# Attention scores with neighbours on partitions, and two gates that each form their own u3 product, in a two-layer graph network

## The chip, the core and the metric

The kernel runs on one core of a Trainium2 chip. The metric is the time of one execution on the device, in microseconds (us). Beside the time of each run there is a profile of one execution, which records what every engine did: TensorE (PE, with its weight loads, PEld), VectorE (DVE), ScalarE (ACT), GpSimd (POOL) and the queues that issue DMAs (SP and ACT here).

## What is computed

The input x holds 32 samples of 512 nodes with 128 features, all in 32-bit floats. One 512 x 512 adjacency matrix of zeros and ones, with a full diagonal, serves all samples. Layer 0 is a graph attention, layer 1 a gated network that runs five steps; both begin with a layer norm and a ReLU, and both add their result to x.

```python
# layer 0
h = relu(layernorm(x)); hw = h @ W
e_src = hw @ a_src; e_dst = hw @ a_dst
logits = leaky_relu(e_src[:, :, None] + e_dst[:, None, :], 0.2)
alpha = softmax(logits + where(A > 0, 0.0, -1e9), axis=-1)
x = x + leaky_relu(alpha @ hw + b, 0.3)
# layer 1: h = relu(layernorm(x)), then five times
m = A @ h                          # the same for both halves of av
u3 = h @ u3_w.T + u3_b
z = sigmoid(av @ w3_w.T + w3_b + u3)
r = sigmoid(av @ w4_w.T + w4_b + u3)
hv = tanh(av @ w5_w.T + w5_b + (r * h @ u5_w.T + u5_b))
h = (1 - z) * h + z * hv
# at last: x = x + h
```

Since in_matrix and out_matrix are the same, both halves of av are m, and the kernel adds the two halves of each weight once at its start. A sigmoid is formed from a tanh of half its argument.

## The kernel before

A sample's 512 nodes lie as 128 partitions of K = 4 nodes each. All matrix work is in 32-bit floats. PSUM is used as eight banks of 128 x 512, handed out in turn under one tag by `bank(name)` (line 62).

The preparation (lines 98 to 170) loads the adjacency matrix and the weights, writes the additive mask of layer 0 with four DVE operations (line 131), turns the matrix into `adjT` with sixteen transposes (line 142) and sums and turns the gate weights (lines 151 to 167). For the gates it forms w4 and, in `w3dT`, the difference of w3 and w4.

`layer0(b)` (lines 202 to 280) is a generator. It does one piece of a sample's layer 0 and gives control back at each `yield`, twelve pieces in all:

- layer norm on DVE, with the inverse root on POOL (`relu_layernorm`, line 177);
- four transposes into one PSUM bank and a copy by ACT (`transposed`, line 194);
- h W with one further column for e_src (line 217), and a product that gives e_dst on every partition (line 222); ACT adds each node's e_src to it, four times 128 x 512 (line 227);
- six pieces (lines 233 to 265) with the nodes that receive on partitions. For each group of 128 nodes: the leaky ReLU (line 237), mask and row maximum in one DVE operation (line 240), its sign turned (line 244), the exponential with its row sum (line 246), four transposes of the result and a copy (lines 197 and 198), and four products with hw (line 258). A group's exponential, transposes and products are one piece apart;
- division by the row sum and bias (line 270), the leaky ReLU and the sum with x (lines 275 and 276);
- the second layer norm, and at the end its transposes.

The main loop (lines 389 to 412) runs 160 passes, one for each sample and step. A pass starts `aggregate` for one item (four products, line 289, and the copy to `mT` by ACT), `gate_r` for the item of the pass before, `candidate` and `update` for the one before that, and then `turn` (four transposes, line 338) for the last. Between these it calls `advance()` three times, and each call does one piece of layer 0 for a sample that is still to come. At most six samples are in the loop (WIDTH); twelve have space for their state (SLOTS). The first six samples go through layer 0 before the loop, two side by side (`start_first`, line 370). When no sample is left for layer 0 the loop runs on alone, and the last two samples alternate.

Both gates need u3 h. `gate_r` starts one PSUM bank with it (line 300), adds w4 m (line 301), and ACT reads the bank for r (line 303). `candidate` then adds (w3 - w4) m to the same bank (line 311), so that ACT reads z from it (line 315). A pass thus has nine products of 512 columns.

The calls are emitted in this order, and the framework's scheduler puts them into one queue per engine. An engine works through its queue in order.

Of the kernel before, what the change touches and what calls it, by code (L numbers as in the profile page):

```python
# [17 lines left out]
NEG = -1000000000.0  # L18
WIDTH = 6
SLOTS = 12  # L20


@with_exitstack
def gat_then_gated_gnn_kernel(
# [29 lines left out]
    const = ctx.enter_context(tc.tile_pool(name="const", bufs=1))  # L54
    state = ctx.enter_context(tc.tile_pool(name="state", bufs=1))
# [28 lines left out]
    mask = const.tile([P, K, N], F32, name="mask")  # L84
    wsrc = const.tile([P, D + 1], F32, name="wsrc")
    wdst = const.tile([P, P], F32, name="wdst")
    bias0 = const.tile([P, D], F32, name="bias0")
    nc.scalar.dma_start(out=bias0, in_=g_b.partition_broadcast(P))
    w3dT = const.tile([P, D], F32, name="w3dT")
# [8 lines left out]
    with tc.tile_pool(name="prep", bufs=1) as prep:  # L98
# [28 lines left out]
        nc.vector.tensor_scalar(wdst, ones, wa[:, 1:2], None, ALU.mult)  # L127


        for k in range(K):  # L130
            nc.vector.tensor_scalar(
                mask[:, k, :].rearrange("p (c q) -> p c q", c=K),
                a_sb[:, k, :].rearrange("p (q c) -> p c q", c=K),
                0.0,
                NEG,
                ALU.is_le,
                ALU.mult,
            )
# [12 lines left out]
        sums = {}  # L151
        for name in ("w4", "w3", "w5"):
            sums[name] = prep.tile([P, D], F32, name=name + "s")
            nc.vector.tensor_tensor(sums[name], wide[name][:, :D], wide[name][:, D:], ALU.add)
        nc.vector.tensor_tensor(sums["w3"], sums["w3"], sums["w4"], ALU.subtract)
        for name, dst in (("w3", w3dT), ("w4", w4sT), ("w5", w5sT)):
            ws = sums[name]
            t_ps = bank(name + "_ps")
            nc.tensor.transpose(t_ps[:, :D], ws, ident)
            nc.vector.tensor_copy(dst, t_ps[:, :D])  # L160
# [13 lines left out]
    hNs = [state.tile([P, K, D], F32, name=f"hN_{s}") for s in range(SLOTS)]  # L174

# [26 lines left out]
    def layer0(b):  # L202
# [9 lines left out]
        hw = w2.tile([P, K, D + 1], F32, tag="hw", name=f"hw_{b}")  # L212
        for half in range(K // 2):
            hp = bank(f"hp_{b}_{half}")
            hp2 = hp[:, : 2 * (D + 1)].rearrange("p (c e) -> p c e", c=2)
            for c in range(2):
                nc.tensor.matmul(  # L217
                    hp2[:, c, :], lhsT=hT[:, ts(2 * half + c, P)], rhs=wsrc, start=True, stop=True
                )
            nc.scalar.copy(hw[:, 2 * half : 2 * half + 2, :], hp2)  # L220
        ed = bank(f"ed_{b}")
        nc.tensor.matmul(ed, lhsT=wdst, rhs=hT, start=True, stop=True)  # L222
        sums = w2.tile([P, K], F32, tag="sums", name=f"sums_{b}")
        s_all = []
        for k in range(K):
            s = w2.tile([P, N], F32, tag=f"s{k}", name=f"s_{b}_{k}", bufs=1)
            nc.scalar.activation(s, ed, AF.Identity, bias=hw[:, k, D : D + 1])
            s_all.append(s)
        yield

        probs, turned = {}, {}
        av = None
        for i in range(K + 2):
            if i < K:
                s = s_all[i]
                lg = w2.tile([P, N], F32, tag="lg", name=f"lg_{b}_{i}")
                nc.vector.scalar_tensor_tensor(lg, s, 0.2, s, ALU.mult, ALU.max)
                ml = w2.tile([P, N], F32, tag="ml", name=f"ml_{b}_{i}")
                top = w3.tile([P, 1], F32, tag="top", name=f"top_{b}_{i}")
                nc.vector.tensor_tensor_reduce(  # L240
                    ml, lg, mask[:, i, :], 1.0, -3.0e38, ALU.add, ALU.max, top
                )
                ntop = w3.tile([P, 1], F32, tag="ntop", name=f"ntop_{b}_{i}")
# [145 lines left out]
    while ready or waiting or coming or current or any(pipeline):  # L389
# [8 lines left out]
        if pipeline[1]:  # L398
            gate_r(*pipeline[1])
# [44 lines left out]
```

## Time and profile before

| what | value |
|---|---|
| time, median of 3 runs (lowest to highest) | 1699.15 us (1698.23 to 1699.98) |
| the profiled execution's own time | 1699.15 us |
| its span, first to last instruction | 1697.2 us |
| mean granted clock of TensorE, as a share of full speed | 0.979 |
| DVE busy | 943.7 us (56%) |
| ACT busy | 706.9 us (42%) |
| POOL busy | 79.3 us (5%) |
| x, one sample's load, issue to landing (median) | 2.6 us |
| out, one sample's store, issue to landing (median) | 2.0 us |

In a line of the groups, the form is: source line, engine, operation, names of output and inputs, shapes, count, then total busy time in us and the mean of one in ns, then idle time ahead of it and what ended it. In a timeline the first two columns are the start and the length in us. The lengths of matmuls overlap[...]. The times in a profile are those of one execution; the prediction is a sum against that execution's time.

### The profile page before, as it was taken

The numbers are of one execution on the slowest core, as the hardware profiler recorded it, in microseconds if no ns is written. First come the engines' busy times: TensorE is split into PE (matmuls) and PEld (weight loads), VectorE is DVE, ScalarE is ACT, GpSimd is POOL, SyncE is SP. The second block draws the span as 40 slices with busy tenths as digits, with TensorE's granted clock in tenths as the row PEclk, the third lists the DMA queues.
The fourth block names the chain that finished last, engine by engine and source line by source line (L and its number), as shares of the span: only waits on it lengthen the run. The fifth ranks groups of instructions, "written<-read, shape, count | busy, mean of one in ns | idle before, by whom it ended". The sixth has DMA issues, their size and how long they took to land.

```text
span 1697.2 us, 15921 instructions
## 1 busy us (share of the span) xinstructions
PE 1597.3 (94%) x5656; PEld 860.7 (51%) x5656; DVE 943.7 (56%) x2455; ACT 706.9 (42%) x1285; POOL 79.3 (5%) x70
## 2 busy tenths in 40 slices
PE   5557999999999999999999999999999999999987
PEld 4444555554555555455555545555554554444433
DVE  5665666664666665466666546666663654433433
ACT  4443444443444443344444334444443443333322
POOL 0000000000000000000000000000000000000000
PEclk9768999999999999999999999999999999999999
DMA  1000000000000000000000000000000000000100
GB/s 60 13 13 13 7 7 8 11 7 7 32 13 7 7 7 7 7 31 13 7 7 7 7 7 31 13 7 7 7 0 7 25 7 0 1 0 0 38 0 13
DMA packets 11456, 19.50 MB, mean 11 GB/s; under 512 B 2161, under 2 KB 3057, under 8 KB 11249
## 3 DMA queue, kind: packets, MB, share of 16 engines
q1 hardware_dynamic: 10080, 18.35, 3.3%
q8 instruction: 44, 0.72, 0.2%
q10 hardware_dynamic: 1296, 0.14, 0.1%
q14 instruction: 36, 0.29, 0.1%
HBM read 10.10 MB, written 8.39 MB: 11 GB/s over the span
## 4 chain that ended last, share of the span: by engine, by line
PE 80%; DVE 14%; POOL 3%; ACT 1%; issue 1%; DMA 0%; POOLq 0%; ACTq 0%
PE m L289 28%; PE v L318 7%; PE g L300 7%; PE v L317 7%; PE g L301 7%; PE av L258 7%; PE g L311 6%; PE h L338 4%; PE t_p L197 4%; POOL rs_b L187 3%; DVE hN L189 2%; DVE o L270 2%; PE hp L217 2%; PE ed L222 2%; DVE st_b L181 1%; DVE x L276 1%
## 5 line engine op out<-in xcount | busy, mean ns | idle before, releaser
L289 PE MATMUL m<-adjT,hN 128*128 128x512 f32 x1280 | 578.1, 594 | 7.4 <-DVE hN L341 7.4
L289 PEld LDWEIGHTS m<-adjT,hN 128*128 128x128 f32 x1280 | 231.5, 191 | 240.2 <-issue 230.9
L305 DVE SCALAR_TENSOR_TENSOR rh<-rs,hT 128x512 f32<-128x512 f32 x160 | 110.2, 689 | 360.3 <-ACT rs L303 360.2
L293 ACT COPY mT<-m 128x512 f32<-128x512 f32 x160 | 93.8, 586 | 503.1 <-PE m L289 503.1
L329 DVE TENSOR_TENSOR d<-hv,hT 128x512 f32<-128x512 f32 x160 | 109.4, 684 | 176.9 <-ACT hv L326 176.9
L303 ACT ACTIVATE rs<-g,rb 128x512 f32<-128x512 f32 x160 | 109.6, 685 | 173.4 <-PE g L301 173.4
L326 ACT ACTIVATE hv<-v,vb 128x512 f32<-128x512 f32 x160 | 110.1, 688 | 148.7 <-PE v L318 148.7
L311 PE MATMUL g<-mT,w3dT 128*128 128x512 f32 x320 | 163.6, 593 | 0.0
L300 PE MATMUL g<-hT,u3T 128*128 128x512 f32 x320 | 163.5, 592 | 0.0
L317 PE MATMUL v<-mT,w5sT 128*128 128x512 f32 x320 | 163.5, 592 | 0.0
L318 PE MATMUL v<-rh,u5hT 128*128 128x512 f32 x320 | 163.4, 592 | 0.0
L301 PE MATMUL g<-mT,w4sT 128*128 128x512 f32 x320 | 163.4, 592 | 0.0
L258 PE MATMUL av<-hw,pt 128*128 128x128 f32 x1024 | 137.6, 279 | 0.0
L258 PEld LDWEIGHTS av<-hw,pt 128*128 128x128 f32 x1024 | 129.5, 196 | 13.0 <-issue 12.7
L315 ACT ACTIVATE zs<-g,zb 128x512 f32<-128x512 f32 x160 | 110.0, 687 | 44.4 <-PE g L311 43.7
L341 DVE COPY hN<-h 128x512 f32<-128x512 f32 x128 | 87.8, 686 | 69.7 <-PE h L338 69.7
L331 DVE SCALAR_TENSOR_TENSOR e<-zs,d 128x512 f32<-128x512 f32 x160 | 110.4, 690 | 3.6
L332 DVE SCALAR_TENSOR_TENSOR hT<-e,hT 128x512 f32<-128x512 f32 x160 | 109.9, 687 | 3.1
L338 PEld LDWEIGHTS h<-ident,hT 128*128 128x128 f32 x640 | 77.2, 141 | 49.9 <-issue 34.7
L197 PEld LDWEIGHTS t_p<-ident,pe 128*128 128x128 f32 x512 | 65.6, 147 | 72.5 <-issue 41.1
L338 PE MATMUL h<-ident,hT 128*128 128x128 f32 x640 | 96.5, 273 | 4.4 <-DVE hT L332 4.4
L301 PEld LDWEIGHTS g<-mT,w4sT 128*128 128x128 f32 x320 | 60.8, 190 | 76.5 <-issue 76.5
(85 smaller groups left out, 1448.3 us busy)
## 6 DMA issues: line engine op xcount, KB each, us to landing
x<-in_x_dram SPq DMA_DIRECT2D x32, 256.0 KB, 2.6
out_dram<-res SPq DMA_DIRECT2D x32, 256.0 KB, 2.0
a_sb<-in_adj_dram SPq DMA_DIRECT2D x1, 1024.0 KB, 8.2
w<-in_L_gnn_w_w_dram SPq DMA_DIRECT2D x3, 128.0 KB, 2.3
u<-in_L_gnn_u_w_dram SPq DMA_DIRECT2D x2, 64.0 KB, 2.3
bias<-in_L_gnn_b_dram ACTq DMA_DIRECT2D x1, 64.0 KB, 6.1
gw<-in_L_gnn_W_dram ACTq DMA_DIRECT2D x1, 64.0 KB, 8.4
cols<-in_L_gnn_w_b_dram ACTq DMA_DIRECT2D x3, 0.5 KB, 6.3
```

Of the source, the lines that this page charges most:

```text
L197: nc.tensor.transpose(t[:, ts(k, P)], src[:, k, :], ident)
L258: nc.tensor.matmul(av[:, ts(k, P)], lhsT=pt[:, ts(c, P)], rhs=hw[:, c, :D], start=(c == 0), stop=(c == K - 1),)
L289: nc.tensor.matmul(m_ps, lhsT=hN[:, k, :], rhs=adjT[:, k, :], start=(k == 0), stop=(k == K - 1))
L300: nc.tensor.matmul(g_ps, lhsT=u3T, rhs=hT, start=True, stop=False)
L301: nc.tensor.matmul(g_ps, lhsT=w4sT, rhs=mT, start=False, stop=True)
L305: nc.vector.scalar_tensor_tensor(rh, r, 1.0, hT, ALU.add, ALU.mult)
L311: nc.tensor.matmul(g_ps, lhsT=w3dT, rhs=mT, start=False, stop=True, skip_group_check=True)
L317: nc.tensor.matmul(v_ps, lhsT=w5sT, rhs=mT, start=True, stop=False)
L318: nc.tensor.matmul(v_ps, lhsT=u5hT, rhs=rh, start=False, stop=True)
L326: nc.scalar.activation(hv, v_ps, AF.Tanh, bias=vb)
L331: nc.vector.scalar_tensor_tensor(e, z, 1.0, d, ALU.add, ALU.mult)
L338: nc.tensor.transpose(t[:, ts(k, P)], hT[:, ts(k, P)], ident)
```

## The change

Layer 0 forms its scores with the sending nodes (the neighbours) on partitions. The logit of a pair is the larger of s and 0.2 s, with s = e_src + e_dst. Its exponential is the larger of exp(s) and exp(0.2 s). Divided by exp(0.2 e_src), which is the same for all neighbours of a node and so cancels in the softmax, it is the larger of exp(0.8 e_src + e_dst) and exp(0.2 e_dst). ACT forms the first for 128 neighbours against all 512 nodes, and the second as one number per neighbour (`low`). One DVE operation takes the larger and multiplies by the transposed adjacency matrix, which is there already for layer 1. The result has the layout that the product with hw needs. The row sums come from a further column of ones in hw, so the products have 130 columns. The row maxima, the mask and the transposes of the scores go. Twelve pieces stay twelve.

The gates form u3 h twice: each gate has its own PSUM bank and its own u3 product, and w3 takes the place of w3 - w4. Both gates are done where r alone was, and `candidate` becomes part of `update`.

The short form of the scores holds for an adjacency matrix of zeros and ones with a neighbour for each node, and for scores that aren't large. The preparation computes from the inputs a flag that says whether this is broken. At the end of the program each engine reads the flag and branches: where it is set, `general_path` computes everything once more, in a loop over the samples, with mask and row maxima.

```diff
-    mask = const.tile([P, K, N], F32, name="mask")
+    wrow = const.tile([P, D + 1], F32, name="wrow")
+    wcol = const.tile([P, P], F32, name="wcol")
+    flag = const.tile([P, 1], mybir.dt.int32, name="flag")
...
-        for k in range(K):
-            nc.vector.tensor_scalar(
-                mask[:, k, :].rearrange("p (c q) -> p c q", c=K),
-                a_sb[:, k, :].rearrange("p (q c) -> p c q", c=K),
-                0.0,
-                NEG,
-                ALU.is_le,
-                ALU.mult,
-            )
+        nc.vector.tensor_copy(wrow[:, :D], gw)
+        nc.vector.tensor_copy(wrow[:, D : D + 1], wa[:, 1:2])
+        nc.vector.tensor_scalar(wcol, ones, wa[:, 0:1], None, ALU.mult)
...
+        odd = prep.tile([P, K, N], F32, name="odd")
+        nc.vector.scalar_tensor_tensor(
+            odd, a_sb, 0.0, a_sb, ALU.not_equal, ALU.not_equal, accum_out=viol[:, 0:1]
+        )
+        nc.vector.tensor_reduce(deg, a_sb, mybir.AxisListType.X, ALU.max)
+        nc.vector.tensor_scalar(bare, deg, 0.0, None, ALU.is_le)
+        nc.vector.tensor_reduce(viol[:, 1:2], bare, mybir.AxisListType.X, ALU.add)
+        nc.vector.tensor_tensor(wa2, wa, wa, ALU.mult)
+        nc.vector.tensor_reduce(viol[:, 2:3], wa2, mybir.AxisListType.X, ALU.add)
+        viol_ps = bank("viol_ps")
+        nc.tensor.matmul(viol_ps[:, 0:3], lhsT=ones, rhs=viol, start=True, stop=True)
+        nc.vector.tensor_scalar(over, viol_ps[:, 2:3], SCORES, None, ALU.is_gt)
+        nc.vector.tensor_reduce(total, viol_ps[:, 0:2], mybir.AxisListType.X, ALU.add)
+        nc.vector.tensor_tensor(total, total, over, ALU.add)
+        nc.vector.tensor_scalar(flag, total, 0.0, None, ALU.is_gt)
...
+    hws = [state.tile([P, K, D + 2], F32, name=f"hw_{s}") for s in range(3)]
+    for t in hws:
+        nc.vector.memset(t[:, :, D + 1 : D + 2], 1.0)
...
-        ed = bank(f"ed_{b}")
-        nc.tensor.matmul(ed, lhsT=wdst, rhs=hT, start=True, stop=True)
-        for k in range(K):
-            nc.scalar.activation(s, ed, AF.Identity, bias=hw[:, k, D : D + 1])
+        es = bank(f"es_{b}")
+        nc.tensor.matmul(es, lhsT=wcol, rhs=hT, start=True, stop=True)
+        low = w2.tile([P, K], F32, tag="low", name=f"low_{b}")
+        nc.scalar.activation(low, hw[:, :, D], AF.Exp, scale=0.2)
         yield
-        for i in range(K + 2):
...
-                nc.vector.tensor_tensor_reduce(
-                    ml, lg, mask[:, i, :], 1.0, -3.0e38, ALU.add, ALU.max, top
-                )
...
-                transposed(pt, probs.pop(i - 1).rearrange("p (c q) -> p c q", c=K), f"p{b}_{i}")
...
-            yield
+        for c in range(K):
+            e = w2.tile([P, N], F32, tag="e0", name=f"e0_{b}_{c}")
+            nc.scalar.activation(e, es, AF.Exp, bias=hw[:, c, D : D + 1], scale=0.8)
+            pt = w2.tile([P, N], F32, tag=f"pt{c}", name=f"pt_{b}_{c}")
+            nc.vector.scalar_tensor_tensor(
+                pt, e, low[:, c : c + 1], adjT[:, c, :], ALU.max, ALU.mult
+            )
+            probs.append(pt)
+            yield
+        for half in range(K // 2):
+            av = bank(f"av_{b}_{half}")
+            av2 = av[:, : 2 * (D + 2)].rearrange("p (c e) -> p c e", c=2)
+            for i in range(2):
+                k = 2 * half + i
+                for c in range(K):
+                    nc.tensor.matmul(
+                        av2[:, i, :],
+                        lhsT=probs[c][:, ts(k, P)],
+                        rhs=hw[:, c, :],
+                        start=(c == 0),
+                        stop=(c == K - 1),
+                    )
+            nc.vector.reciprocal(rsum[:, 2 * half : 2 * half + 2], av2[:, :, D + 1])
+            for i in range(2):
+                k = 2 * half + i
+                nc.vector.scalar_tensor_tensor(
+                    o[:, k, :], av2[:, i, :D], rsum[:, k : k + 1], bias0, ALU.mult, ALU.add
+                )
+            yield
...
-    def gate_r(b, step):
+    def gate(b, step):
         hT, mT = hTs[b % SLOTS], aggregates[b]
-        g_ps = bank(f"g_{b}_{step}")
-        nc.tensor.matmul(g_ps, lhsT=u3T, rhs=hT, start=True, stop=False)
-        nc.tensor.matmul(g_ps, lhsT=w4sT, rhs=mT, start=False, stop=True)
+        for name, wT, bias, pool in (("r", w4sT, rb, w2), ("z", w3sT, zb, w3)):
+            g_ps = bank(f"{name}_{b}_{step}")
+            nc.tensor.matmul(g_ps, lhsT=u3T, rhs=hT, start=True, stop=False)
+            nc.tensor.matmul(g_ps, lhsT=wT, rhs=mT, start=False, stop=True)
+            g = pool.tile([P, N], F32, tag=name, name=f"{name}s_{b}_{step}")
+            nc.scalar.activation(g, g_ps, AF.Tanh, bias=bias, scale=0.5)
...
-    def candidate(b, step):
-        nc.tensor.matmul(
-            g_ps, lhsT=w3dT, rhs=mT, start=False, stop=True, skip_group_check=True
-        )
...
+    ctx.close()
+    general = nc.values_load(flag[0:1, 0:1])
+    with tc.If(general > 0):
+        with ExitStack() as inner:
+            general_path(
+                inner,
+                tc,
+                x,
+                adj,
+                (ident, wsrc, wdst, bias0, w3sT, w4sT, w5sT, u3T, u5hT, zb, rb, vb),
+                out,
+            )
```

The new function, cut to its frame:

```python
def general_path(ctx, tc, x, adj, ws, out):
    ...
    with tc.For_i(0, B, 1) as b:
        nc.sync.dma_start(out=xb, in_=...)
        relu_layernorm(h, xb, "a")
        ...
        for i in range(K):
            ...
        for step in range(STEPS):
            ...
        nc.sync.dma_start(out=..., in_=hN)
```

## The prediction

> **What bounds the kernel now.** I read the page's busy shares first, then the groups by line, then busy time by stage, and last the timeline of each stage.
>
> ```profile
> span 1697.2 us, 15921 instructions
> ...
> PE 1597.3 (94%) x5656; PEld 860.7 (51%) x5656; DVE 943.7 (56%) x2455; ACT 706.9 (42%) x1285; POOL 79.3 (5%) x70
> ...
> PEclk9768999999999999999999999999999999999999
> ```
>
> TensorE (PE) is busy 94% of the span, so what the change does to PE decides, unless a stage waits for something else. PEclk is full from the fourth slice on; only the start runs at a reduced clock.
>
> ```profile
> L289 PE MATMUL m<-adjT,hN 128*128 128x512 f32 x1280 | 578.1, 594 | 7.4 <-DVE hN L341 7.4
> ...
> L300 PE MATMUL g<-hT,u3T 128*128 128x512 f32 x320 | 163.5, 592 | 0.0
> ...
> L258 PE MATMUL av<-hw,pt 128*128 128x128 f32 x1024 | 137.6, 279 | 0.0
> ...
> L197 PE MATMUL t_p<-ident,pe 128*128 128x128 f32 x512 | 81.1, 284 | 13.5 <-ACT pe L246 13.5
> ```
>
> x1280 for the 640 products of line 289 shows that each f32 product is two MATMUL records, and a transpose (line 197) is one. The mean of a record, 592 ns, is not its price in a stream, since records overlap. The price is read from start to start in the timeline of a steady stretch:
>
> ```profile
> 258.90 0.66 PE L197 MATMUL t_b<-ident,hN 128*128 128x128 f32 x4 [0.65 <-DVE hN L192]
> 259.39 0.60 PE L338 MATMUL h<-ident,hT 128*128 128x128 f32 x4
> 259.83 3.60 PE L289 MATMUL m<-adjT,hN 128*128 128x512 f32 x8
> 263.27 1.02 PE L300 MATMUL g<-hT,u3T 128*128 128x512 f32 x2
> 264.12 1.02 PE L301 MATMUL g<-mT,w4sT 128*128 128x512 f32 x2
> ...
> 274.48 0.60 PE L197 MATMUL t_p<-ident,pe 128*128 128x128 f32 x4
> 274.92 1.02 PE L311 MATMUL g<-mT,w3dT 128*128 128x512 f32 x2
> ...
> 277.93 1.06 PE L258 MATMUL av<-hw,pt 128*128 128x128 f32 x8
> 278.82 0.60 PE L338 MATMUL h<-ident,hT 128*128 128x128 f32 x4
> ```
>
> From 263.27 to 264.12 one product of 512 columns takes 0.86 us; four of them (line 289) 3.44; four transposes 0.44 (274.48 to 274.92); four products of 128 columns 0.89 (277.93 to 278.82), so 0.22 each. Nothing stands idle but 0.65 us before t_b, which waits for VectorE (DVE).
>
> By stages:
>
> ```profile
> 0.00:140.57 140.57, 72.91 (x421) 62.30 (x421) 84.96 (x338) 58.52 (x124) 14.47 (x19) 0.77 0.10 30
> 140.57:391.71 251.14, 247.12 (x920) 135.25 (x920) 150.67 (x422) 114.88 (x216) 15.55 (x13) 0.99 0.02 7
> 391.71:416.21 24.50, 24.50 (x68) 11.44 (x67) 10.10 (x15) 7.95 (x13) 0.00 (x0) 1.00 0.00 1
> 416.21:1614.15 1197.94, 1183.74 (x4072) 620.88 (x4071) 669.07 (x1638) 504.39 (x902) 49.25 (x39) 1.00 0.03 11
> 1614.15:1697.20 83.05, 69.06 (x180) 30.79 (x180) 28.87 (x43) 21.19 (x32) 0.00 (x0) 0.98 0.02 7
> ```
>
> Columns are stage, its length, then busy time of PE, PE's weight loads, DVE, ScalarE (ACT), GpSimd (POOL), then clock and DMA. The start (0 to 140.57) keeps PE half busy at clock 0.77. From there to 1614.15 PE is full at a full clock. From 391.71 to 416.21 no layer-0 work runs: three passes of the main loop take 24.50, so 8.17 each, which is nine products (7.73) and four transposes (0.44). With layer 0 beside it, the chain of waits shows the same POOL line at 214.19, 255.66 and 297.13: one sample of layer 0 per four passes, in 41.47 us. The sum 140.57 + 26 x 41.47 + 48 x 8.17 = 1611 against 1614.15 confirms this division (26 samples are left after the first six; 160 passes less 104 and less 8 in the end). In the end two samples alternate, and a round takes 19.3 us, in which PE also waits:
>
> ```profile
> 1633.53 3.70 PE L289 MATMUL m<-adjT,hN 128*128 128x512 f32 x8 [1.00 <-DVE hN L341]
> ...
> 1647.13 1.02 PE L318 MATMUL v<-rh,u5hT 128*128 128x512 f32 x2
> ...
> 1652.83 3.70 PE L289 MATMUL m<-adjT,hN 128*128 128x512 f32 x8 [1.00 <-DVE hN L341]
> ```
>
> And in the start two samples go through layer 0 side by side; from the first score operation to the sum with x is 21.8 us (65.52 to 87.34), 21.0 for the third pair (108.62 to 129.65):
>
> ```profile
> 65.52 2.42 ACT L227 ACTIVATE s<-ed,hw 128x512 f32<-128x512 f32 x4 [1.12 <-PE ed L222]
> ...
> 87.34 0.68 DVE L276 TENSOR_TENSOR x<-x,o 128x512 f32<-128x512 f32 x1
> ```
>
> [...]
>
> **The change part by part.**
>
> *The second u3 product.* Each of 160 passes gets one more 512-column product. In 48 free passes nothing else changes: 48 x 0.86 = +41.3. The other engines follow: DVE has five and ACT four operations of 0.69 in a pass of 9.03.
>
> *Layer 0 in 26 periods.* Added: four products, 3.44. Removed: sixteen transposes of scores in four groups, 4 x 0.44 = 1.76. The sixteen products for the output go from 128 to 130 columns: 0.22 x 2/128 x 16 = 0.06. Products of 129 columns (line 217) already take 0.89 for four, as those of 128 do, so an odd width has no price. Sum +1.74. The 0.65 before t_b: t_b waits for the second layer norm, whose DVE chain begins when the last output product ends. The built order keeps between the two one aggregate, four gate products and two of the candidate, 3.44 + 6 x 0.86 = 8.6 us of PE, as before, but only two of the four operations on the output (0.3 each) remain behind that product, because the other half comes earlier. So the wait shrinks to between 0 and 0.65; I take -0.25. But this wait can grow too, if an operation of the main loop (0.69) is put into that chain: rh is one, in the built order it stands ahead of the ReLU; the upper end is +1. Taken: +1.5 per period, 26 x 1.5 = +39.
>
> *Work off PE that goes.* Per sample DVE loses 4 x (0.68 + 0.69 + 0.08 + 0.15) and gets 4 x 0.69; ACT loses four biased copies, four evacuations and the sums, and keeps four exponentials of about 0.69. DVE was busy 121 of 200 us and ACT 92, both beside a full PE: worth nothing in these periods. The four exponentials stand together in ACT's built order, and the third waits until DVE has used the first (two buffers). Behind them ACT holds the copy of the aggregate, needed by PE one pass later (9 us), and DVE holds rh, also needed a pass later: hidden. A PSUM bank returns after eight requests; the fuller loop asks 27 times per period instead of 26, and the scores' bank is read within the four exponentials, so I see no wait there.
>
> *The end.* In a round PE now does both gates of both samples before the first candidate. The loop from candidate (1647.13) to the next aggregate (1652.83) stays 5.70, and three added products lie ahead of it (the u3 products of both, and the second sample's z moved forward): +2.58 a round for three rounds, and +1.72 at the last, where the second sample ends the kernel: +9.5.
>
> *The start.* The score stage of a pair is now a chain of eight exponentials and eight multiplications that alternate over two buffers. ACT and DVE both take 0.69, and the rhythm comes to about 0.7 us each; the second sample's scores product comes 1.75 after the first (0.89 + 0.86). First exponential to last multiplication: about 7.2. Then PE has twenty output products left, of which fifteen lie ahead of the first sample's second half: 3.3 at full clock, 6.6 at half. Reciprocal, two operations and the leaky ReLU, 0.17 + 0.6 + 0.7 = 1.5. In all 12 to 15 against 21.0 and 21.8: 6 to 10 less for a pair; taken 8[...]. Layer norms, loads and transposes of x between pairs stay (19 us from 89.45 to 108.62). The first pair pays for the preparation: the mask (2.17) goes; two passes over 2048 columns come. No row shows them; the nearest is 0.61 per 512 columns, so 2.5 and about 2.2. About ten small operations of 0.1 to 0.3 follow, and the built order puts all of these ahead of the first normalisation on DVE, which came at 13.80 and will come near 20.5; its successors were held by PE until 19.35 anyhow. Net +4.5 (3 to 6). Together 4.5 - 3 x 8 = -19.5, with ends -9 and -27.
>
> *The flag and the branch.* For these inputs it is false: the matrix holds 0 and 1 with a full diagonal, and the squared sum of the two score vectors is near 128 x 2 x 0.01 = 2.6, below 25; so the general path costs only its skipping. Every engine reads the flag and branches at the end of its queue. [...] Taken +2.
>
> *At no cost.* The three hw tiles and the memsets (before x has landed at 6.6), the small exponential (ahead of its scores product on ACT), the same DMAs in SP's queue, POOL unchanged.
>
> *Sum.* 41.3 + 39 + 9.5 - 19.5 + 2 = +72.3. The profiled execution took 1699.15 with a span of 1697.2, and is the median of the runs shown; so 1771.
>
> **Rivals.** *The start gives nothing back*: half clock throughout and a longer preparation. For it: clock 0.53 at 100 to 110; against: DVE and ACT have 12 us less in each pair's stage. 1771 + 19 = 1790.
> *A new wait in each period*: ACT stops in the middle of its exponentials for DVE, and something behind it reaches PE late. For it: strict order in both queues; against: a slack of a pass. At 1.5 us: 26 x 1.5 = +39, 1810.
> *Faster*: the removed transposes were worth their records' 273 ns each and not 0.11, because each group interrupts the stream. Then 416 of them give 113.6 rather than 45.8, and 1771 - 68 = 1703, with the start at its best (-27) 1696. It decides from 1.14 us for a group of four on. Against: groups of 0.44 in the timeline at every place.
> *The skip is dear*[...]: +20, 1791.
>
> **How the numbers follow.** Forecast 1771: 0.70; start gives nothing back 0.12; new wait 0.10; skip dear 0.05; faster 0.03. A measurement of this kernel tells 0.2% (3.4 us). Unknowns about the forecast: start -8 to +10, the wait before t_b -10 to +26, the end of the program -2 to +4: 1755 to 1798 covers the forecast, the first rival and the dear skip; the new wait and the faster case stay out. Faster by over 0.2%: 0.02; within: 0.01; slower: 0.97.
>
> **What would show it.** Lines for u3 with 640 records; a free pass of 9.03 us; a period near 43.0; a round near 21.9; the first aggregate near 121. Wrong if periods are under 41.5, if PE has idle time before the gates, or if the general path's lines appear in the trace.

## The result and the profile after

| | before | after |
|---|---|---|
| time, median (lowest to highest), 4 runs each | 1698.95 us (1698.23 to 1699.98) | 1757.76 us (1756.75 to 1758.56) |
| ratio to before, 95% interval | | 1.0345 (1.0327 to 1.0363) |
| span of the profiled execution | 1697.2 us | 1755.3 us |
| first aggregate of the main loop starts at | 140.57 us | 119.64 us |
| a free pass (no layer 0 beside it) | 8.17 us | 9.02 us |
| a period (one sample of layer 0, four passes) | 41.47 us | 42.30 us |
| a round of the end | 19.3 us | 21.8 us, two of 23.4 us |

The kernel became 3.5% slower, 58.8 us by the medians and 58.1 by the spans. The forecast was 1771 with a range of 1755 to 1798. The direction and the place of the loss were right; the loss was forecast 13 us too large. Where a time stands below without a range, that kernel ran once; those with a range ran four or five times and spread by at most 2.6 us.

The page of the profile after:

```profile
span 1755.3 us, 14839 instructions
...
PE 1674.0 (95%) x5466; PEld 870.1 (50%) x5466; DVE 886.1 (50%) x2115; ACT 568.4 (32%) x933; POOL 65.1 (4%) x70
...
PEclk9679999999999999999999999999999999999998
...
L457 PE MATMUL r<-mT,w4sT 128*128 128x512 f32 x320 | 163.4, 592 | 0.0
L456 PE MATMUL r<-hT,u3T 128*128 128x512 f32 x320 | 163.4, 592 | 0.0
L456 PE MATMUL z<-hT,u3T 128*128 128x512 f32 x320 | 163.4, 592 | 0.0
L457 PE MATMUL z<-mT,w3sT 128*128 128x512 f32 x320 | 163.4, 592 | 0.0
```

DVE has lost 58 us of work and ACT 139, and the kernel is slower all the same: the engine that counts, PE, has 77 us more. Line 456, the u3 product, stands there twice with 320 records each, 640 in all. The last digit of PEclk is an 8 where before had a 9: the end of the kernel now has something that slows TensorE.

The same stages as before (stage, length, then busy time of PE, weight loads, DVE, ACT, POOL, clock, DMA):

```profile
0.00:119.64 119.64, 59.31 (x326) 48.49 (x327) 74.85 (x284) 31.67 (x58) 13.18 (x19) 0.78 0.12 34
119.64:377.68 258.04, 257.31 (x874) 135.94 (x874) 139.69 (x356) 89.82 (x151) 12.70 (x13) 0.99 0.02 7
377.68:404.75 27.07, 27.07 (x73) 12.57 (x73) 10.10 (x15) 7.95 (x13) 0.00 (x0) 1.00 0.00 1
404.75:1657.70 1252.95, 1250.87 (x4000) 637.73 (x4000) 632.69 (x1418) 417.80 (x681) 39.25 (x39) 1.00 0.03 10
1657.70:1755.30 97.60, 79.46 (x196) 35.34 (x196) 28.78 (x43) 21.19 (x32) 0.00 (x0) 0.93 0.02 6
```

The start is 20.9 us shorter. The loop, from the first aggregate to the end rounds, has grown from 1473.58 to 1538.06, +64.5; the end from 83.05 to 97.60, +14.5. Together +58.1. In the three free passes PE is busy 27.07 of 27.07. The new thing is the second row: PE is busy 257.31 of 258.04, where before had 247.12 of 251.14. The same holds for the fourth row (2.1 us idle, 14.2 before). So an idle time of PE that stood in every period of before is gone. The list of waits (who waited, for whom, us in total, times, longest) shows which. Before, then after:

```profile
PE t_b L197 <- DVE hN L192: 46.4, 31, 7.9
```

```profile
PE t_b L365 <- DVE hN L360: 28.3, 6, 7.2
```

Six of these waits belong to the six samples of the start. The other 25 of before, one in nearly every period, do not exist any more.

How the layer norm that t_b waits for lies in each kernel is read in the timeline (start, length, engine; only lines of that chain are kept). Before, the last output product having ended at 290.7:

```profile
294.86 0.69 DVE L276 TENSOR_TENSOR x<-x,o 128x512 f32<-128x512 f32 x1
...
297.10 0.68 DVE L305 SCALAR_TENSOR_TENSOR rh<-rs,hT 128x512 f32<-128x512 f32 x1
297.13 1.50 POOL L187 TENSOR_TENSOR rs_b<-ve_b,mhalf 128x4 f32<-128x4 f32 x1 [34.14 <-DVE ve_b L185]
...
299.91 0.41 DVE L192 TENSOR_SCALAR hN<-hN 128x512 f32<-128x512 f32 x1
...
300.38 0.66 PE L197 MATMUL t_b<-ident,hN 128*128 128x128 f32 x4 [0.65 <-DVE hN L192]
```

After, where it ended at 231.9:

```profile
234.73 0.69 DVE L431 TENSOR_TENSOR x<-x,o 128x512 f32<-128x512 f32 x1
...
237.00 1.01 POOL L355 TENSOR_TENSOR rs_b<-ve_b,mhalf 128x4 f32<-128x4 f32 x1 [37.36 <-DVE ve_b L353]
...
239.28 0.68 DVE L463 SCALAR_TENSOR_TENSOR rh<-rs,hT 128x512 f32<-128x512 f32 x1
239.87 0.42 DVE L360 TENSOR_SCALAR hN<-hN 128x512 f32<-128x512 f32 x1
...
240.73 0.60 PE L365 MATMUL t_b<-ident,hN 128*128 128x128 f32 x4
```

From the end of the output products to the end of the ReLU it is 9.6 us before (290.7 to 300.32) and 8.4 after (231.9 to 240.29). PE has the same work in between in both: a turn 0.44, an aggregate 3.44, six products 5.16, together 9.0. So before t_b came 0.8 us late in each period (the product ahead of it started at 298.71 and a stream would have gone on at 299.57; as idle time 0.65 is shown). In after its input is done 0.44 us ahead of it: its bracket has no wait. The 1.2 us are made of 1.3 less for outputs behind the last product, 0.5 less on GpSimd (1.50 to 1.01), and 0.6 more because rh now stands ahead of the ReLU.

### The profile page after: what moved, and what is told of

Its sections match the earlier page's. It is cut to its first block, busy times and chain, and to the rows that moved or that the text cites. A ratio compares the mean times of both kernels' runs of the same rounds, so it can differ in the third digit from the quotient of the medians.

```text
span 1755.3 us, 14839 instructions
## 1 busy us (share of the span) xinstructions
PE 1674.0 (95%) x5466; PEld 870.1 (50%) x5466; DVE 886.1 (50%) x2115; ACT 568.4 (32%) x933; POOL 65.1 (4%) x70
## 4 chain that ended last, share of the span: by engine, by line
PE 94%; DVE 4%; POOL 1%; ACT 1%; DMA 0%; issue 0%; ACTq 0%; POOLq 0%; DVEq 0%
PE m L444 32%; PE r L456 8%; PE r L457 8%; PE z L457 8%; PE z L456 8%; PE v L470 8%; PE v L471 8%; PE av L414 6%; PE h L485 4%; PE hp L385 2%; PE es L390 2%; PE t_a L365 1%; PE t_b L365 1%; DMA gw<-in_L_gnn_W_dram 0%; DVE pt L401 0%; DVE hN L357 0%
## 5 line engine op out<-in xcount | busy, mean ns | idle before, releaser
L459 ACT ACTIVATE rs<-r,rb 128x512 f32<-128x512 f32 x160 | 109.9, 687 | 180.9 <-PE r L457 180.9
L457 PE MATMUL r<-mT,w4sT 128*128 128x512 f32 x320 | 163.4, 592 | 0.0
L456 PE MATMUL r<-hT,u3T 128*128 128x512 f32 x320 | 163.4, 592 | 0.0
L456 PE MATMUL z<-hT,u3T 128*128 128x512 f32 x320 | 163.4, 592 | 0.0
L457 PE MATMUL z<-mT,w3sT 128*128 128x512 f32 x320 | 163.4, 592 | 0.0
L459 ACT ACTIVATE zs<-z,zb 128x512 f32<-128x512 f32 x160 | 110.0, 687 | 164.7 <-PE z L457 164.7
L414 PEld LDWEIGHTS av<-hw,pt 128*128 128x128 f32 x1024 | 124.2, 190 | 33.8 <-issue 25.1
L414 PE MATMUL av<-hw,pt 128*128 128x130 f32 x1024 | 127.3, 276 | 4.7 <-DVE pt L401 3.9
L401 DVE SCALAR_TENSOR_TENSOR pt<-e,low,adjT 128x512 f32<-128x512 f32 x128 | 90.6, 747 | 30.5 <-ACT e L399 27.3
```

Source lines behind the costliest of these rows:

```text
L414: nc.tensor.matmul(av2[:, i, :], lhsT=probs[c][:, ts(k, P)], rhs=hw[:, c, :], start=(c == 0), stop=(c == K - 1),)
L456: nc.tensor.matmul(g_ps, lhsT=u3T, rhs=hT, start=True, stop=False)
L457: nc.tensor.matmul(g_ps, lhsT=wT, rhs=mT, start=False, stop=True)
L459: nc.scalar.activation(g, g_ps, AF.Tanh, bias=bias, scale=0.5)
```

## Experiments

In what follows "the product theory" is that of the prediction: the loss is PE's second u3 product, and the new layer 0 is a gain. "The chain theory" came from the result: the wait before t_b is decided by a few tenths of the DVE chain against the work that PE has between.

### The two halves of the change apart: e1_gates_once and e2_old_scores

The new layer 0 with the gates of before:

```diff
-        for name, wT, bias, pool in (("r", w4sT, rb, w2), ("z", w3sT, zb, w3)):
-            g_ps = bank(f"{name}_{b}_{step}")
-            nc.tensor.matmul(g_ps, lhsT=u3T, rhs=hT, start=True, stop=False)
-            nc.tensor.matmul(g_ps, lhsT=wT, rhs=mT, start=False, stop=True)
...
+        nc.tensor.matmul(g_ps, lhsT=u3T, rhs=hT, start=True, stop=False)
+        nc.tensor.matmul(g_ps, lhsT=w4sT, rhs=mT, start=False, stop=True)
...
+    def candidate(b, step):
...
+        nc.tensor.matmul(
+            g_ps, lhsT=w3dT, rhs=mT, start=False, stop=True, skip_group_check=True
+        )
```

> The new scores of layer 0 with the gates of before (u3 h summed once, w3 - w4 added in the candidate). Product theory: what the change lost is the price of 160 products of 0.86 us on a full PE, and the new scores by themselves gain. Then a free pass is 8.17 us, a period of four passes 42.30 - 3.44 = 38.9 and up to 0.4 more, because only five products instead of six now lie between the last output product and t_b; the start stays near 119.6; in all about 1622 us. Scores rival: the new scores cost as much as they save, and the start alone gains; then about 1680. Order rival (both gates in one place cost by their order): also about 1622, so this run does not tell it from the first.

Measured: 1628.01 us (1626.40 to 1629.00), ratio to before 0.9582 (0.9566 to 0.9598). The new layer 0 alone makes the kernel 4.2% faster. First aggregate at 119.1, free pass 8.17, rounds of 19.3 as before. 1622 was expected, with a period of 38.9 to 39.3. The period is 39.45, and the wait before t_b is back:

```profile
PE t_b L371 <- DVE hN L366: 38.0, 30, 7.2
```

Thirty waits, six of the start and 24 in the loop, of 0.40 each. PE's products of a period sum to 38.86 (the 42.30 of after, which has no wait, less four u3 products of 0.86), so a wait that is shown as 0.40 lengthens the period by 0.59: the shown idle time begins at the end of the last record (1.02 us after its start), while a stream would have gone on after 0.86.

The old layer 0 with the gates of after (and without the check of the inputs):

```diff
-        if pipeline[1]:
-            gate_r(*pipeline[1])
+        if pipeline[1]:
+            gate(*pipeline[1])
         advance()
         if pipeline[2]:
-            candidate(*pipeline[2])
             update(*pipeline[2])
```

> The scores, mask and transposes of before with the gates of after (two u3 products), no flag. Product theory: a period 41.47 + 3.44 = 44.9 us, with the wait before t_b unchanged at 0.65, since six products lie between as before; a free pass 9.02; rounds at the end as in after (21.8); start 140; about 1843 us. If the second product were partly hidden in waits of the old layer 0, the period would stay under 44.3 and the time under 1827.

Measured: 1847.35 us, 4 more than expected. Free pass 9.02, period 44.97, and a wait before t_b of 0.73 to 0.74 in the periods. The u3 product costs 148 us with the old layer 0 and 130 with the new one (1757.76 less 1628.01). The loss of the change is therefore the gates alone, and the product theory stands. What the gates cost depends on whether the wait before t_b stays (with the old scores it even grows, 0.65 to 0.74) or is covered by the longer stream of products (with the new scores).

### The product or the order of the gates: e8_z_without_u3

The gates of after stay where they are, but u3 h is left out of z.

```diff
-            nc.tensor.matmul(g_ps, lhsT=u3T, rhs=hT, start=True, stop=False)
-            nc.tensor.matmul(g_ps, lhsT=wT, rhs=mT, start=False, stop=True)
+            if name == "r":
+                nc.tensor.matmul(g_ps, lhsT=u3T, rhs=hT, start=True, stop=False)
+            nc.tensor.matmul(g_ps, lhsT=wT, rhs=mT, start=(name == "z"), stop=True)
```

> After, with the u3 product left out of the gate z (z is then formed from w3 m alone); order of the gates, banks and all else as in after. Product theory: 160 products less, 160 x 0.86 = 138 us less than after, give or take 10 for waits that come back before t_b: about 1622. Order rival: the order and the banks of the two gates hold part of the loss, so it stays above 1640.

Measured: 1631.07 us, within 3.1 us of e1_gates_once, with the same free pass (8.17), period (39.45) and wait (0.40). So doing both gates early, with a bank for each, costs nothing by itself in the loop; the product does. In the end the order has a price: an undisturbed round takes 20.1 us here and 19.3 in e1_gates_once. The time is 126.7 us less than after, where 160 x 0.86 = 138 was expected: with one product fewer between the last output product and t_b, the wait came back in 24 periods, 24 x 0.59 = 14 us.

### The chain before t_b: e5_outputs_late and e7_turn_later

First, the chain is made longer in after: all four outputs wait for the second half.

```diff
-            nc.vector.reciprocal(rsum[:, 2 * half : 2 * half + 2], av2[:, :, D + 1])
-            for i in range(2):
-                k = 2 * half + i
...
+            parts.append(av2)
+            nc.vector.tensor_copy(total4[:, 2 * half : 2 * half + 2], av2[:, :, D + 1])
             yield
+        nc.vector.reciprocal(rsum, total4)
+        for k in range(K):
```

> After, but the reciprocal of the row sums is taken once for both halves, so that all four operations on the output wait for the second half. Chain theory of the wait before t_b: in after, t_b would start at 240.73 and its input is done at 240.29, a slack of 0.4; two operations of 0.26 and a reciprocal moved behind the last output product lengthen the chain by about 0.7, so a wait of 0.2 to 0.4 us comes back in each period, 5 to 10 us in all: about 1765. Rival: the wait went because GpSimd's operation takes 1.01 instead of 1.50 us, and the split of the outputs has no part in it: no wait, 1758.

Measured: 1773.96 us, 16.2 more than after. The wait stands in the periods again, 0.40 as shown, and the period is 42.89 (+0.59). From the first aggregate to the first round of the end it is 14.0 us more than in after; the first aggregate comes 1.2 later, and one more aggregate of the end is lengthened, by 1.7 (see below). The direction is the chain theory's. The size is outside what was expected, because the expectation counted the wait at its shown length, 0.2 to 0.4, and a shown 0.40 costs 0.59. GpSimd's operation stays at 1.006 us here, so that a slower GpSimd is not what brings the wait back.

Then PE gets more to do before t_b. To e1_gates_once, which has the wait, one more `yield` is added, so the transposes come one piece of layer 0 later and a sample takes thirteen pieces (its periods vary from 40.6 to 42.7 us).

```diff
         relu_layernorm(hNs[b % SLOTS], x1, f"b{b}")
         yield
+        yield
         transposed(hTs[b % SLOTS], hNs[b % SLOTS], f"b{b}")
```

> The kernel of e1 with one more piece in layer 0, between the second layer norm and its transposes, so that more products stand ahead of t_b. Chain theory of the wait before t_b: in e1 only five products lie between the last output product and t_b and a wait of 0.40 us is shown in 24 periods, at 0.59 us of period each. With more of them ahead, the wait goes in most periods: 8 to 14 us less than e1, 1614 to 1620. Rival: the wait is of another kind (a PSUM bank, GpSimd) and stays, 1626 to 1630.

Measured: 1612.81 us (1612.02 to 1614.55), ratio to before 0.9494 (0.9480 to 0.9509).

```profile
PE t_b L371 <- DVE hN L366: 28.3, 6, 7.2
```

Only the six waits of the start are left, and the kernel is 15.2 us faster than e1_gates_once. In the profiled executions the loop is 14.1 shorter, and 24 waits of 0.59 are 14.2. No operation was added or taken away. The chain theory is shown from both sides: a longer chain brings the wait, more work of PE in front of it takes it away.

### What the check costs: e3_no_check, e6_check_late, e10_check_out, e11_check_in_loop, e12_check_split

e3_no_check is after without the flag, the reading of it and the general path (it leaves these out).

```diff
-        odd = prep.tile([P, K, N], F32, name="odd")
...
-        nc.vector.tensor_scalar(flag, total, 0.0, None, ALU.is_gt)
...
-    general = nc.values_load(flag[0:1, 0:1])
-    with tc.If(general > 0):
```

> After without the check of the inputs, the flag, the branch and the general path. Start theory: the check's operations on VectorE hold the first normalisations, so that the first pair's scores came 5 us later than in before; without them the first aggregate comes 4 to 6 us sooner (about 114.6), and the end of the program is 1 us shorter; the loop is unchanged. About 1751 us against 1757.8. Rival: the delay comes from the order that PE keeps in the preparation and not from the check, then the start moves by less than 2 us and the time is 1755 or more. Dear-skip rival: the branch holds more than 5 us at the end of the program, which would then go.

Measured: 1750.71 us (1750.22 to 1751.68), ratio to before 1.0305 (1.0291 to 1.0319), so 7.05 less than after. The first aggregate starts at 113.95, 5.7 earlier, and the time from the end of the last sum to the end of the span is 2.9 as in before, where after has 3.9: the skip costs 1.0 us, the preparation 5.7. The reason for the second is in the timeline of after: on DVE the two passes over the adjacency matrix stand ahead of the first normalisation, which before began at 13.80.

```profile
10.89 2.28 DVE L297 SCALAR_TENSOR_TENSOR odd<-a_sb 128x2048 f32<-128x2048 f32 x1
...
13.30 2.27 DVE L301 TENSOR_REDUCE deg<-a_sb 128x4 f32<-128x2048 f32 x1
...
19.24 1.10 DVE L357 TENSOR_SCALAR h<-x,mv_a,rs_a 128x128 f32<-128x128 f32 x4
```

The next four start from e1_gates_once or e7_turn_later and try to win these 5.7 us with the check kept. In e6_check_late its code is moved behind the six samples of the start.

```diff
     waiting.extend(start_first())
+    viol = late.tile([P, 3], F32, name="viol")
...
+    nc.vector.tensor_scalar(flag, total, 0.0, None, ALU.is_gt)
```

> The kernel of e1 (new scores, u3 h summed once) with the check of the inputs moved behind the layer 0 of the first six samples in the program. Same start theory: 4 to 6 us less than e1, 1622 to 1624 us. Rival: 1626 or more.

Measured: 1625.63 us (1625.04 to 1627.62), ratio 0.9567 (0.9552 to 0.9582): not separable from e1_gates_once (1626.40 to 1629.00). The first aggregate is at 120.33, later than there. The place in the program was not the place in the queue:

```profile
20.34 0.59 DVE L340 TENSOR_SCALAR h<-x,mv_a,rs_a 128x128 f32<-128x128 f32 x2
20.85 2.28 DVE L527 SCALAR_TENSOR_TENSOR odd<-a_sb 128x2048 f32<-128x2048 f32 x1
...
23.06 0.42 DVE L343 TENSOR_SCALAR h<-h 128x512 f32<-128x512 f32 x1
23.39 2.28 DVE L531 TENSOR_REDUCE deg<-a_sb 128x4 f32<-128x2048 f32 x1
```

`odd` depends on nothing that the six samples make, and the scheduler put it between the second sample's normalisation and its ReLU.

In e10_check_out, made from e7_turn_later, the check first gets a copy from sample 5, so that it can't run before.

```diff
+    nc.vector.tensor_copy(viol[:, 0:1], x1s[5][:, 0, 0:1])
     odd = late.tile([P, K, N], F32, name="odd")
...
+    nc.vector.tensor_copy(deg, x1s[5][:, :, 0])
     nc.vector.tensor_reduce(deg, a_sb, mybir.AxisListType.X, ALU.max)
```

> As e7 (the shared u3 product with the new scores, and the turn of the layer-0 result one piece later), but the two passes over the adjacency matrix and the small steps behind them now read or overwrite something that sample 5 leaves behind in layer 0, so that they cannot stand in the preparation. Start theory: the first aggregate comes 5 to 6 us earlier than in e7 (near 114, as in the kernel without the check), the periods keep their length, and the two passes (2.3 us each on VectorE) cost at most 2 us where they stand: 1607 to 1609 us. Rival, that the end of the program and not the preparation made e3 faster: first aggregate unchanged, 1612.8 us.

Measured: 1611.70 us (1610.84 to 1612.17), ratio 0.9485 (0.9470 to 0.9501), 1.1 less than e7_turn_later, with ranges that touch. The copy bound the check to the very moment that the last layer norm of the start needs DVE:

```profile
110.99 2.29 DVE L529 SCALAR_TENSOR_TENSOR odd<-a_sb 128x2048 f32<-128x2048 f32 x1
111.22 2.91 POOL L338 TENSOR_TENSOR rs_b<-ve_b,mhalf 128x4 f32<-128x4 f32 x1 [2.31 <-DVE ve_b L336]
...
114.18 1.11 DVE L340 TENSOR_SCALAR hN<-x,mv_b,rs_b 128x128 f32<-128x128 f32 x4 [0.89 <-POOL rs_b L338]
115.21 2.28 DVE L534 TENSOR_REDUCE deg<-a_sb 128x4 f32<-128x2048 f32 x1
117.40 0.41 DVE L343 TENSOR_SCALAR hN<-hN 128x512 f32<-128x512 f32 x1
...
117.96 1.09 PE L348 MATMUL t_b<-ident,hN 128*128 128x128 f32 x4 [6.14 <-DVE bare L536]
...
119.13 5.62 PE L428 MATMUL m<-adjT,hN 128*128 128x512 f32 x8
```

Up to `odd` everything comes 5.0 to 5.4 us earlier than in e7_turn_later, and here it is lost again. The second line is the more telling: GpSimd's operation, 1.01 us in e7_turn_later, takes 2.91 beside `odd`. (The bracket of t_b names `bare`; the operation it needs is the ReLU in front of it.)

In e11_check_in_loop the copies come from the state that pass 146 of the loop has updated, where no layer 0 is left.

> As e10, but the two passes over the adjacency matrix and the small steps behind them overwrite something that pass 146 of the main loop leaves behind, where no layer 0 is left and VectorE is busy some 3.5 of 8.2 us. In e10 they stood in front of the last layer norm of the start, and the GpSimd operation beside the first of them took 2.91 us in place of 1.01. Start theory: first aggregate near 114 (5 to 6 us earlier than in e7), nothing lost in the loop but up to 1 us where the passes stand: 1607 to 1609 us. If the first aggregate is early and the time stays at 1612, the gain is lost again in the loop.

Measured: 1616.05 us (1615.79 to 1616.72), ratio 0.9517 (0.9501 to 0.9533): slower than e7_turn_later. The first aggregate is at 113.89, 6.1 earlier, as the start theory has it, but the waits of PE have a new line:

```profile
PE viol_ps L563 <- DVE viol L558: 7.2, 1, 7.2
```

The check's product with three columns was put into PE's queue ahead of the next pass, and PE stood 7.2 us while DVE did the two passes over the matrix. Behind this wait the granted clock is 0.50 from 1466.5 to 1473.4 us, so that the next aggregate takes 4.57 us in place of 3.6. The expectation named a cost of up to 1 us on DVE and left out who waits behind the small product. In e12_check_split the passes are held to passes 144 and 146, and the sum and the product to pass 149, by a copy from an aggregate:

```diff
+            if passes == 144:
+                nc.vector.tensor_copy(viol[:, 0:1], hTs[pipeline[2][0] % SLOTS][:, 0:1])
...
+            if passes == 146:
+                nc.vector.tensor_copy(deg, hTs[pipeline[2][0] % SLOTS][:, 0:K])
...
+            if passes == 149:
+                nc.vector.tensor_copy(viol[:, 2:3], aggregates[pipeline[0][0]][:, 0:1])
```

> As e11, but the check is in three parts, held back to passes 144, 146 and 149 of the main loop, and the small product of the check is held to pass 149, so that it no longer stands in TensorE's queue in front of work while VectorE is still in the two long passes. In e11 the first aggregate came 6.1 us earlier than in e7, and TensorE then stood 7.2 us before that small product. Start theory: first aggregate near 114, no wait of TensorE before the small product over 1 us, no later start of the end than in e7 less 5 us: 1606 to 1608 us. If a part of the check still holds TensorE in the loop, up to 1612.

Measured: 1607.86 us (1607.31 to 1608.78), ratio to before 0.9466 (0.9450 to 0.9482). The first aggregate is at 114.16, and the product no longer waits:

```profile
1485.75 1.02 PE L457 MATMUL v<-rh,u5hT 128*128 128x512 f32 x2
1486.61 0.28 PE L566 MATMUL viol_ps<-viol,ones 128*128 128x3 f32 x2
1486.75 0.64 PE L477 MATMUL h<-ident,hT 128*128 128x128 f32 x4
```

This kernel has the new layer 0, its general path, and u3 h summed once. It is 5.3% faster than before and 8.5% faster than after (1607.86 to 1757.76).

### The end: e9_end_filled

In the end of after two of the aggregates take 5.3 and 5.4 us where all others take 3.7. From the timeline of PE:

```profile
1678.03 0.66 PE L485 MATMUL h<-ident,hT 128*128 128x128 f32 x4 [1.37 <-DVE hT L479]
1679.47 3.70 PE L444 MATMUL m<-adjT,hN 128*128 128x512 f32 x8 [0.78 <-DVE hN L488]
...
1699.82 0.66 PE L485 MATMUL h<-ident,hT 128*128 128x128 f32 x4 [1.37 <-DVE hT L479]
1701.26 5.32 PE L444 MATMUL m<-adjT,hN 128*128 128x512 f32 x8 [0.79 <-DVE hN L488]
```

In both rounds PE is idle for 1.37 us before the turn and for 0.78 after it. Before had 0.45 and 1.00, because there the second sample's z came after the first sample's candidate and filled the first gap. In the traces of before and after the granted clock changes only at times that lie whole multiples of 3.41 us apart, and the two drops here, to 0.50, last one such stretch each. With the stretch ahead of each of three aggregates, in the columns of the stages:

```profile
1677.24:1680.66 3.42, 1.85 (x7) 1.09 (x8) 3.20 (x5) 0.14 (x1) 0.00 (x0) 1.00 0.00 0
1680.66:1684.07 3.41, 2.94 (x10) 1.26 (x8) 0.51 (x2) 0.59 (x1) 0.00 (x0) 1.00 0.00 0
1697.72:1701.14 3.42, 1.39 (x6) 0.42 (x4) 3.13 (x6) 0.69 (x1) 0.00 (x0) 1.00 0.00 0
1701.14:1704.55 3.41, 3.29 (x4) 1.51 (x5) 1.36 (x3) 0.00 (x0) 0.00 (x0) 0.50 0.00 0
1721.62:1725.03 3.41, 1.26 (x6) 0.72 (x6) 3.12 (x6) 0.69 (x1) 0.00 (x0) 1.00 0.00 0
1725.03:1728.45 3.42, 3.42 (x5) 1.35 (x4) 0.88 (x2) 0.00 (x0) 0.00 (x0) 0.50 0.00 0
```

Where PE was busy for 1.85 us of a stretch, the clock stayed full in the next; where for 1.39 or 1.26, it was half. To test that the idle time is the cause, a product that nothing uses is put into the gap; it reads the first sample's hv.

```diff
+        if b == B - 2 and step > 0:
+            fill = bank(f"fill_{b}_{step}")
+            nc.tensor.matmul(fill, lhsT=u3T, rhs=hv, start=True, stop=True)
         d = w2.tile([P, N], F32, tag="d", name=f"d_{b}_{step}")
```

> After, with one unused product of 512 columns in each of the last rounds, which reads the candidate's tanh of the first of the two samples and so falls into the idle 1.3 us of PE. Clock theory of the end: two of the rounds in after take 23.4 instead of 21.8 us because PE idles longer ahead of the turn and its clock is halved for the start of the next aggregate; with the gap filled all rounds take 21.8, 3 us less than after, about 1754.5. Rival: the longer aggregates have another cause and stay: 1758 to 1760.

Measured: 1755.27 us, 2.5 less than after, with more work for PE; from the first round of the end on it is 1.6 less in the profiled executions.

```profile
1697.56 1.12 PE L477 MATMUL fill<-hv,u3T 128*128 128x512 f32 x2 [0.84 <-ACT hv L473]
1700.24 0.60 PE L488 MATMUL h<-ident,hT 128*128 128x128 f32 x4
1701.62 3.70 PE L444 MATMUL m<-adjT,hN 128*128 128x512 f32 x8 [0.78 <-DVE hN L491]
```

All aggregates of the end take 3.70 now. A round takes 22.1, 0.3 more than after's undisturbed 21.8, since the first turn starts behind the filling product. From 170 us to the kernel's last turn, PE is now busy for at least 2.20 us of every stretch. In after the drop to 0.50 at 1701.14 came behind a stretch that was 59% idle (1.39 us busy of 3.42), and the longest single idle time in it was 1.37 us.

The traces also show why only some of the like rounds are hit. A round of 21.8 us is not a multiple of 3.41, so that its idle times fall into one stretch in one round and astride two in another. In before and after, from 170 us on, when the start's changes are over, each stretch at full clock with PE busy for 1.39 us or less (three in after, one in before) was followed by a clock of 0.50, and none with 1.85 or more; before has 1.96 at the least until its last turn. In e8_z_without_u3 an aggregate of 5.21 us follows a stretch in which PE was busy for about 1.60. No run moved a round against these stretches on purpose.

## Why the prediction was right, and where it was off

By the steps of its sum, against what was measured (spans; the end of the loop is the start of the first end round):

| step | forecast | measured |
|---|---|---|
| 48 free passes | +41.3 | +40.8 (9.02 - 8.17 each) |
| 26 periods | +39 | +23.7 (the rest of the loop's +64.5; 26 x 0.83 is 21.6 of it) |
| start | -19.5 | -20.9 |
| end rounds | +9.5 | +13.5 |
| flag and branch | +2 | +1.0 |
| sum | +72.3 | +58.1 |

*The second u3 product* was priced rightly: 0.86 from start to start, and free passes of 9.02. The price held because PE was already at its limit there (busy for 27.07 of 27.07 us in three free passes); e8_z_without_u3 and e1_gates_once show that the product and not the new order of the gates is what costs.

*The periods* hold the mis-sized term. The products and transposes of layer 0 were counted rightly: four passes at 9.02, 0.88 for two groups of transposes, 0.89, 0.86 and 3.58 for layer 0's products make 42.29, and the period is 42.30. The term that failed is the wait before t_b, for which the prediction took -0.25 of a range from 0 to -0.65. It went wholly, and it was worth more than its shown 0.65: some 0.8 from start to start. That is 0.55 to 0.6 per period, 14 to 15 us in all, about the 14.2 by which the sum missed; the other misses, +4.0 at the end and -0.5 to -1.4 for the passes, the skip and the start, nearly cancel. The prediction had the mechanism, two outputs earlier and rh ahead of the ReLU, but not the sizes. For the outputs it took 0.6 less, where 1.3 was measured, and for rh it allowed 0.69 more, where it is 0.6. GpSimd's operation, which it called unchanged, became 0.5 shorter. Together 1.2 us, more than the 0.8 there was to win; and it took the shown idle time as the most that could be won. Its 8.6 us of PE's work left out the turn of 0.44, which stands in both kernels and changes nothing between them. e5_outputs_late and e7_turn_later show how sharp this edge is: 0.44 us of slack, and 14 us when it is gone.

*The start.* The score stage of the second pair fell from 21.8 to 12.4 us, within the 12 to 15 of the forecast. The preparation costs 5.25 at the first score operation and 5.7 at the first aggregate, where 4.5 was taken, with `odd` at 2.28 and `deg` at 2.27 against 2.5 and 2.2. One end of its range was not the sum of its parts: 6 less three times 6 is -12, not -9. The 8 taken for a pair, from 6 to 10, was the author's estimate; the mean granted clock of the start is 0.78, and 0.77 in before, where it was 0.50 from 50 to 60 us with PE busy for 3.26 us. The rival that the start gives nothing back fell.

*The end.* A round without a disturbed aggregate takes 21.8; 21.9 was forecast. Not foreseen was that the longer idle time before the turn, 1.37 for 0.45, would bring TensorE's clock down to 0.50: 1.6 us in each of two rounds, 3.3 of the 4.0 us by which this term missed.

*The skip* costs 1.0 us by e3_no_check, and no line of the general path stands in the trace. The +2 taken for it and the +20 of the rival of a dear skip were the author's estimates, which no trace of before shows; that rival fell. The rival of a new wait in each period fell also; PE waits for nothing in the periods. The faster rival, transposes that would be worth more than 0.11 each, fell with the period that equals the sum of its products.

So the time was inside the range, on its lower part, for the reason given, less one wait. That the misses beside this wait nearly cancel is luck.

## What to carry to other kernels

Where an engine is full, price an added operation from start to start in its stream (0.86 us here, for a pair of records of 1.02), and a wait likewise; the shown idle time understates it (0.40 shown for 0.59 in e1_gates_once). For each wait that stands in every round, write down both sides, the waiting engine's work in between and the chain it waits for, to the last small operation: a slack of some tenths (0.44 us in after), once lost, costs its overshoot in each round (0.59 us in e5_outputs_late), and moving one call by one piece may win it back (15.2 us in e7_turn_later). Moving code in the program need not move it in a queue, as e6_check_late shows (`odd` at 20.85 us); a dependency holds it there. Then look at what stands behind its smallest instruction on every engine that it touches (7.2 us of PE in e11_check_in_loop).

## What was not expected of the hardware

GpSimd's operation on 128 x 4 numbers takes 1.01 to 1.02 us in all 64 cases of after, but 1.50 in 25 periods of before, where it begins 0.03 us behind the start of rh (0.68 us on VectorE, two inputs), and 2.91 in e10_check_out, where it begins 0.24 behind the start of `odd` (2.29 us, two inputs). In both it ends 0.86 us after the VectorE operation. In before at 176.93 it takes 1.37; it begins 0.19 behind the start of `e` (0.69, two inputs) and ends 0.87 after it. Batch-norm operations of VectorE beside it, in after at 237.00, leave it at 1.01. Where GpSimd began first, 0.16 us ahead of rh (before, at 173.16) or 0.09 ahead of `odd` (after, at 10.80), neither took longer: 1.01 and 0.68, 1.02 and 2.28. But in before at 10.75, where it began 0.08 ahead of the four operations that write the mask (2.17 us together, one input each), it took 2.30. No run changed this alone, so what makes it longer is not shown.

TensorE's clock fell to 0.50 within a stream that was never idle for more than 1.37 us at a time, behind stretches of 3.41 us in which PE was busy for 1.39 and 1.26; an aggregate then took 5.3 to 5.4 us in place of 3.7, and one filling product removed it.
